# A mixer and mixture-of-experts kernel on one core: gate projection as one batch in other banks, output projection in two halves, the last units summed on VectorE, expert weights issued later, new due times

## The chip, the cores and the metric

The kernel runs on one core of a Trainium2 chip. The metric is the device time of one execution in microseconds (us). Five engines work side by side and each executes its own instructions in order: TensorE (PE in the profile; its weight loads are PEld), VectorE (DVE), ScalarE (ACT), GpSimd (POOL) and SyncE (SP), which here only issues transfers. Transfers (DMAs) run apart from the engines, once issued.

## The reference

The input is 16 sequences of 256 positions and 256 features, all float32. Cut to what matters:

```python
x = L0_attn_input_states                       # 16 x 256 x 256
xn = _layernorm(x, axis=-1)
x = x + _L0_attn_ref(xn, ...) + _L0_ffn_ref(xn, ...)

# _L0_attn_ref, a state-space mixer: E = 512 channels, N = 16 states, TR = 128
hidden, gate = jnp.split(jnp.einsum('blh,he->bel', input_states, W_in), 2, axis=1)
hidden = silu(depthwise_conv(hidden, conv_kernel) + conv_bias)       # 4 taps, causal
dt, Bm, Cm = jnp.split(hs_ble @ W_x, [TR, TR + N], axis=-1)
dts = softplus(dt @ W_dt + b_dt)
dA, dBu = exp(dts * A), dts * Bm * hs_ble
state = a * state + bu;  y = einsum('ben,bn->be', state, c)          # scan over positions
y = (scan_out + hidden * D) * silu(gate)
return jnp.einsum('bel,eh->blh', y, W_out)

# _L0_ffn_ref, 32 experts of width 96; the 8 largest router weights are kept
acc + ((silu(x @ wg) * (x @ wu)) @ wd) * w_e
```

## The kernel before

**Tiling.** A sequence (`b`, 0 to 15) is handled as a whole. Its normalized input is kept transposed (`xnT`: features on partitions, 256 positions along the free axis). Two branches read it.

The *mixer* branch: `project` makes the hidden half (4 blocks of 128 channels, in two calls), `conv_first` and `conv_rest` the convolution, `activate` its SiLU, `params` and `widen` and `steps` the step sizes. Its B and C rows go through DRAM (`keep_params`) and come back copied to all partitions (`fetch`, tile `rep`, three buffers). Then 16 units follow, 8 groups of two states (`g`) by 2 halves of the channels (`u`). A unit `k` is: `feed` on GpSimd (L622), for each of its two blocks `decay` on ScalarE (L636), `scan` on VectorE (L644) and `read` on VectorE (L654), and `collect` (L659), a GpSimd-issued transfer that adds the unit's product `pr` to the accumulator `y` as it lands. After the last group `fold` (GpSimd, L667) adds y's two states, `gate` (TensorE, L675) and `gate_silu` (ScalarE, L684) make the gate, `gated` (GpSimd, L689) multiplies, `project_out` (TensorE, L696) projects and `finish` (VectorE, L713) adds the result to the output tile.

The *expert* branch: all 32 experts are computed as 24 blocks of 128 rows, in 12 pairs `q`. `gates` makes two pairs at a time (L469, tile `pg`), `silu` (L482) empties both, `ups` makes one pair (L469, tile `pu`), `weigh` (GpSimd, L488) applies router weights that were spread over partitions (`spread`, L455), `combine` (VectorE, L492) multiplies with the ups, and `down` (L504) accumulates the pair into one PSUM bank `acc`. `settle` (L709) adds that to the output tile, `store` (L717) writes it.

**PSUM banks.** They are rings: two banks `g`, two banks `u`, one `acc`, three for the scan's `da`. A step that takes a bank waits for the bank's owner two turns earlier. In the kernel before the g banks serve `gates`, the first half of `project` and of `widen`, the router's products, `params` and a few small ones; the u banks serve `ups`, the second half of `project` and of `widen`, `turn`, `gate` and `project_out`.

**Order.** Nothing is scheduled by the chip. A planner written into the kernel (`Plan`, L20 to L117) plays the engines forward in time at build: each step has an engine, a length, steps that it needs, ring buffers that it takes and gives, and a due time; a free engine takes the ready step with the smallest due time. The order it arrives at is the program order of each engine. ScalarE needs another function table for exp, SiLU, softplus and square root; a step that needs no change of table counts as due `STAY` us earlier. `early` keeps a step from being planned sooner than so long before it is due. Due times are one base per sequence (`ORIGIN + PERIOD * b` for the mixer, `ORIGIN + LEAD + RATE * b` and a share of it for the experts) plus an offset per kind of step (`DUE`, and `FIRST` for sequence 0). Times in the plan only make the order: on the chip a step runs when its engine reaches it and what it waits for is done.

The weights are loaded once and stay. `load_experts` (L286, L282) loads the experts' weights in four parts of 8 experts, each part in three kinds, 20 transfers on SyncE's queue in all.

Of the kernel before, what the change touches and what calls it, by code (L numbers as in the profile page):

```python
# [19 lines left out]
class Plan:  # L20
# [10 lines left out]
    STAY = 3.0  # L31
# [89 lines left out]
def mamba_moe_kernel(  # L121
# [57 lines left out]
    ORIGIN = 6.0  # L179
    PERIOD = 81.5  # L180
    RATE = 82.5

    DUE = dict(
        load_x=-118.0, stats=-76.5, root=-82.5, invert=-118.5, norm=-68.5, turn=-129.0,
        keep_turned=-72.0, route=-80.5, largest=-63.5, expo=-63.5, choose=-77.0,
        turn_weights=-84.5, keep_weights=-110.5, project=-56.5, conv_first=-44.5, conv_rest=-58.5,
        activate=-57.5, params=-66.0, keep_params=-43.5, widen=-53.0, steps=-31.5, skip=-22.0,
        clear=-38.5, inputs=-11.5, fetch=17.0, feed=-4.5, decay=-6.5, scan=8.5, read=-14.6,
        collect=3.5, spread=2.0, gates=-16.5, ups=10.5, silu=2.5, weigh=-3.5, combine=-3.0,
        down=17.0, settle=76.0, gate=60.0, gate_silu=36.0, fold=84.0, gated=88.5, project_out=84.5,  # L190
        load_again=87.5, finish=40.5,
    )
    EARLY = dict(
        load_x=59.0, stats=5.0, turn=45.0, route=11.0, project=19.0,
# [3 lines left out]
        route=5.0, largest=-13.0, expo=-10.0, choose=-13.0, turn_weights=-18.0, keep_weights=-10.0,  # L198
        project=-4.0, conv_first=3.5, conv_rest=-16.0, activate=-20.0, params=-10.5,
        keep_params=-12.0, widen=-23.0, steps=-0.5, skip=17.5, clear=1.0, inputs=21.5, fetch=8.0,  # L200
        feed=-6.0, decay=-3.0, scan=3.0, read=-6.0, collect=2.5, spread=-10.5, gates=-2.5,
        ups=-5.5, silu=2.5, weigh=2.0, combine=10.0, down=-0.5,
    )
    LEAD = -8.0
# [459 lines left out]

    def fold(b, u):
        y = live["y", b, u]
        nc.gpsimd.tensor_add(y[:, :, 0, :], y[:, :, 0, :], y[:, :, 1, :])  # L667


    def gate(b, q):  # L670
        xs = live["xnT", b]
        pg = bank(f"pgate_{b}_{q}", "u").rearrange("p (j l) -> p j l", j=2)
        for j in range(2):
            for hc in range(HC):
                nc.tensor.matmul(  # L675
                    pg[:, j, :], win_sb[:, hc, E + (2 * q + j) * P : E + (2 * q + j + 1) * P],
                    xs[:, hc, :],
                    start=(hc == 0), stop=(hc == HC - 1),
                )
# [243 lines left out]
```

## Time and profile before

| | |
|---|---|
| time, median of 3 runs (lowest to highest) | 1373.9 us (1372.63 to 1378.73) |
| time of the profiled execution | 1376.13 us |
| span of the profile, first to last instruction | 1374.3 us |
| granted TensorE clock, mean over the span | 0.988 |
| TensorE matmuls busy | 1307.1 us, 6000 instructions |
| VectorE busy | 1161.8 us |
| ScalarE busy | 1125.8 us |
| GpSimd busy | 1191.5 us |

Each float32 matmul stands as two instructions in the profile, so one `ups` or one `down` (4 matmuls) is a row of x8, one `gates` (8 matmuls) a row of x16. In answers on groups and waits a line of the kernel and its tiles name the step (`pu<-xnT,wu_sb` at L469 is `ups`). A wait is written "who waits <- what it waited for: us in all, times, longest". In the timeline a row is its start, its duration, the engine and the step, with the idle time of the engine before it in brackets.

### The profile page before, as it was taken

What the parts mean: (1) busy time and instruction counts of PE and PEld (TensorE: products, weight loads), DVE (VectorE), ACT (ScalarE), POOL (GpSimd) and SP (SyncE); (2) the same over time, 40 slices, a digit from 0 to 9 for tenths busy, and PEclk for the clock granted to TensorE, in tenths of its full rate; (3) what the DMA queues carried; (4) which work ended last, traced back from release to release, by engine and by line L of the source; (5) the groups of instructions that cost most, each with busy time, mean ns of one, the idle gap of its engine ahead of it and who ended that gap; (6) DMA issues with size and microseconds to landing.
All of it is one profiled execution on the core that took longest, in us unless ns stands there. A gap on an engine that the chain in (4) does not pass through costs nothing.

```text
span 1374.3 us, 18848 instructions
## 1 busy us (share of the span) xinstructions
PE 1307.1 (95%) x6000; PEld 1111.7 (81%) x6000; DVE 1161.8 (85%) x1729; ACT 1125.8 (82%) x1905; POOL 1191.5 (87%) x839
## 2 busy tenths in 40 slices
PE   7898899999999999999999999999999999999997
PEld 5777777787788888878888888888888888888875
DVE  2598878988899798888989888898888989888984
ACT  4688798697988979888888988879798887988863
POOL 0688978888899899989898998989899898998985
PEclk8999999999999999999999999999999999999997
DMA  8998978889889989998899999899998999988895
GB/s 247 257 223 176 230 164 196 188 204 220 177 194 225 193 198 214 203 206 184 208 215 208 195 205 203 203 210 212 201 202 195 206 205 214 200 211 191 193 223 100
DMA packets 165875, 278.22 MB, mean 202 GB/s; under 512 B 33008, under 2 KB 99600, under 8 KB 165776
## 3 DMA queue, kind: packets, MB, share of 16 engines
q0 software_dynamic: 36864, 134.23, 51.3%
q1 hardware_dynamic: 126272, 142.74, 37.8%
q8 instruction: 47, 0.77, 0.2%
q10 hardware_dynamic: 2640, 0.05, 0.1%
q14 instruction: 52, 0.43, 0.1%
HBM read 137.51 MB, written 5.24 MB: 104 GB/s over the span
## 4 chain that ended last, share of the span: by engine, by line
POOL 29%; DVE 18%; DMA 15%; PE 12%; ACT 11%; issue 10%; SPq 4%; POOLq 0%; ACTq 0%; DVEq 0%
POOL bu L622 11%; POOL sg L488 8%; DVE da L644 7%; DMA rep<-bcd 7%; POOL y L659 5%; DVE hs L536 4%; DVE pr L654 4%; ACT da L636 4%; PE pu L469 3%; DMA y<-pr 3%; SPq L455 3%; PE acc L504 3%; DMA wr<-wd 3%; POOL y L667 2%; PE pg L469 2%
## 5 line engine op out<-in xcount | busy, mean ns | idle before, releaser
L622 POOL TENSOR_TENSOR bu<-rep,hs 128x1024 f32<-128x1024 f32 x256 | 717.2, 2990 | 113.2 <-DVE da L644 72.2
L644 DVE TENSOR_TENSOR_SCAN da<-da,bu 128x512 f32<-128x512 f32 x512 | 607.9, 1217 | 83.3 <-ACT da L636 56.1
L636 ACT ACTIVATE da<-dts,a_sb 128x256 f32<-128x256 f32 x1024 | 470.9, 473 | 145.6 <-DVE pr L654 124.6
L469 PE MATMUL pu<-xnT,wu_sb 128*128 128x256 f32 x1536 | 362.2, 383 | 24.0 <-ACT gs L684 15.3
L659 POOL DMA_DIRECT2D y<-pr x256 | 360.4, 1413 | 15.8 <-DVE pr L654 7.3
L504 PE MATMUL acc<-wd_sb,h 128*128 128x256 f32 x1536 | 361.6, 379 | 3.3 <-DVE h L492 3.0
L469 PE MATMUL pg<-xnT,wg_sb 128*128 128x256 f32 x1536 | 351.4, 382 | 13.2 <-DVE hs L536 4.8
L469 PEld LDWEIGHTS pu<-xnT,wu_sb 128*128 128x128 f32 x1536 | 291.0, 191 | 70.2 <-ACT gs L684 20.2
L469 PEld LDWEIGHTS pg<-xnT,wg_sb 128*128 128x128 f32 x1536 | 292.0, 191 | 59.8 <-ACT da L636 7.9
L654 DVE TENSOR_TENSOR pr<-da,rep 128x512 f32<-128x512 f32 x512 | 333.3, 676 | 7.3 <-DMA y<-pr 5.2
L488 POOL TENSOR_TENSOR sg<-sg,wr 128x512 f32<-128x512 f32 x192 | 309.2, 1949 | 34.6 <-DMA wr<-wd 33.7
L504 PEld LDWEIGHTS acc<-wd_sb,h 128*128 128x128 f32 x1536 | 290.1, 190 | 44.3 <-DVE h L492 4.7
L492 DVE TENSOR_TENSOR h<-pu,sg 128x512 f32<-128x512 f32 x192 | 130.9, 682 | 75.8 <-PE pu L469 37.9
L636 ACT ACT_TABLE_LOAD x140 | 179.6, 1283 | 2.5
L482 ACT ACTIVATE sg<-pg 128x512 f32<-128x512 f32 x192 | 104.3, 593 | 6.4 <-PE pg L469 3.9
L482 ACT ACT_TABLE_LOAD x82 | 105.2, 1283 | 1.5
L536 DVE SCALAR_TENSOR_TENSOR hs<-ph,small,hs 128x255 f32<-128x255 f32 (+2 forms) x192 | 88.7, 478 | 11.2 <-ACT hs L527 6.6
L696 PE MATMUL po<-wout_sb,y 128*128 128x256 f32 x256 | 63.9, 405 | 8.2 <-POOL y L689 8.2
L667 POOL TENSOR_TENSOR y<-y 128x512 f32<-128x512 f32 x32 | 65.2, 2038 | 1.2 <-DMA y<-pr 1.2
L689 POOL TENSOR_TENSOR y<-y,gs 128x512 f32<-128x512 f32 x32 | 65.8, 2075 | 0.2
L696 PEld LDWEIGHTS po<-wout_sb,y 128*128 128x128 f32 x256 | 51.4, 204 | 17.4 <-POOL y L689 10.0
L551 PE MATMUL px<-hs,wx_sb 128*32 128x256 f32 (+1 forms) x256 | 63.1, 395 | 2.3 <-ACT wT L439 2.3
(64 smaller groups left out, 809.2 us busy)
## 6 DMA issues: line engine op xcount, KB each, us to landing
y<-pr POOLq DMA_DIRECT2D x256, 512.0 KB, 7.4
rep<-bcd SPq DMA_DIRECT2D x128, 512.0 KB, 6.2
wr<-wd SPq DMA_DIRECT2D x128, 192.0 KB, 4.7
wr<-wd SPq DMA_DIRECT2D x128, 128.0 KB, 5.9
wr<-wd SPq DMA_DIRECT2D x128, 64.0 KB, 5.1
xt<-L_attn_input_states_dram SPq DMA_DIRECT2D x16, 256.0 KB, 8.0
o<-L_attn_input_states_dram SPq DMA_DIRECT2D x16, 256.0 KB, 7.5
out_dram<-o SPq DMA_DIRECT2D x16, 256.0 KB, 6.3
```

The lines of the kernel that those rows point to most:

```text
L469: nc.tensor.matmul(p[:, j, :], w[:, hc, ts(c, P)], xs[:, hc, :], start=(hc == 0), stop=(hc == HC - 1),)
L482: nc.scalar.activation(sg, live.pop(("g", b, q)), AF.Silu)
L488: nc.gpsimd.tensor_mul(sg, sg, wr[:, r : r + 2, :])
L492: nc.vector.tensor_mul(h, live.pop(("u", b, q)), live.pop(("sg", b, q)))
L504: nc.tensor.matmul(acc[:, s, :], h[:, j, ts(s, P)], wd_sb[:, c, :], start=(c == 0 and s == 0), stop=(c == FC - 1), skip_group_check=True,)
L536: nc.vector.scalar_tensor_tensor(cv[:, c, k:], ph[:, j, : L - k], cw[:, c, KC - 1 - k : KC - k], cv[:, c, k:], op0=ALU.mult, op1=ALU.add,)
L622: nc.gpsimd.tensor_mul(bu, live["rep", b, g][:, 0:1].to_broadcast([P, CPU, NG, L]), live["hs", b][:, ts(u, CPU), :].unsqueeze(2).to_broadc ...
L636: nc.scalar.activation(da[:, i, :], dts[:, c, :], AF.Exp, scale=a_sb[:, c, n : n + 1])
L644: nc.vector.tensor_tensor_scan(flat, flat, live["bu", k][:, j].rearrange("p n l -> p (n l)"), 0.0, op0=ALU.mult, op1=ALU.add,)
L654: nc.vector.tensor_mul(live["pr", k][:, j], live.pop(("da", m)), live["rep", b, g][:, 1])
L659: nc.gpsimd.dma_start(live["y", b, u].rearrange("p c n l -> p (c n l)"), live.pop(("pr", k)).rearrange("p c n l -> p (c n l)"), accum_op=A ...
L696: nc.tensor.matmul(po[:, s, :], y[:, c % CPU, 0, ts(s, P)], wout_sb[:, c, :], start=(c == 0), stop=(c == EC - 1),)
```

## The change

- `gate` is one step of both halves, 16 matmul instructions, and takes the two g banks in place of two u banks one after the other; `gate_silu` empties both banks in one step.
- `project_out` is two steps, one for each half of the channels, 8 matmul instructions each, in the same bank. Except for the last sequence, the first half still needs both `gated` steps. The order of accumulation inside is by channel block, then by position half.
- In the last sequence and the last group (two units), `collect` is no transfer: VectorE adds the two states of `pr` and adds the sum to `y`, and `gated` is on VectorE too. `fold` then comes ahead of that and needs only the group before.
- `load_experts` is due about 22 us later (the first at 0.6 where it was at -22.0), at the pace of the experts (RATE), and may not be planned more than 1 us before it is due.
- The second halves of `project` and `widen` are planned behind the first.
- `STAY` goes from 3.0 to 10.6; bases and all offsets of the due times are other numbers, and the last sequence has offsets of its own (`LAST`).

```diff
-    STAY = 3.0
+    STAY = 10.6
...
-    ORIGIN = 6.0
-    PERIOD = 81.5
-    RATE = 82.5
+    ORIGIN = 3.0
+    PERIOD = 81.9
+    RATE = 82.3
...
-        clear=-38.5, inputs=-11.5, fetch=17.0, feed=-4.5, decay=-6.5, scan=8.5, read=-14.6,
-        collect=3.5, spread=2.0, gates=-16.5, ups=10.5, silu=2.5, weigh=-3.5, combine=-3.0,
-        down=17.0, settle=76.0, gate=60.0, gate_silu=36.0, fold=84.0, gated=88.5, project_out=84.5,
-        load_again=87.5, finish=40.5,
...
+        clear=-29.0, inputs=-48.5, fetch=-80.5, feed=-8.5, decay=-1.5, scan=3.0, read=-126.1,
+        collect=-35.5, spread=-43.5, gates=-54.0, ups=64.5, silu=5.0, weigh=-76.0, combine=-3.0,
+        down=64.5, settle=-53.5, gate=39.5, gate_silu=95.5, fold=97.0, gated=11.0,
+        project_out=65.5, load_again=45.0, finish=4.0,
     )
     EARLY = dict(
-        load_x=59.0, stats=5.0, turn=45.0, route=11.0, project=19.0,
+        load_x=43.0, load_experts=1.0, stats=5.0, turn=43.0, route=125.0, project=149.0,
     )
...
+    LAST = dict(
+        fetch=64.5, feed=83.5, decay=37.0, scan=-2.5, read=-160.5, collect=-14.0, spread=53.0,
+        gates=7.5, ups=210.0, silu=46.5, weigh=277.0, combine=-108.5, down=-39.5, settle=62.0,
+        gate=-7.0, gate_silu=-383.5, fold=314.5, gated=6.0, project_out=-95.5, finish=14.0,
+    )
-    LEAD = -8.0
+    LEAD = -2.4
...
+    def collect_last(k):
+        b, g, u = unit(k)
+        pr, y = live.pop(("pr", k)), live["y", b, u]
+        nc.vector.tensor_add(pr[:, :, 0, :], pr[:, :, 0, :], pr[:, :, 1, :])
+        nc.vector.tensor_add(y[:, :, 0, :], y[:, :, 0, :], pr[:, :, 0, :])
+
+    def gated_last(b, q):
+        y = live["y", b, q][:, :, 0, :]
+        nc.vector.tensor_mul(y, y, live.pop(("gs", "gate", b, q)))
...
-    def gate(b, q):
+    def gate(b):
         xs = live["xnT", b]
-        pg = bank(f"pgate_{b}_{q}", "u").rearrange("p (j l) -> p j l", j=2)
...
+        for q in range(EC // 2):
+            pg = bank(f"pgate_{b}_{q}", "g").rearrange("p (j l) -> p j l", j=2)
...
-    def project_out(b):
-        po = bank(f"po_{b}", "u").rearrange("p (s h) -> p s h", s=SPS)
-        for s in range(SPS):
-            for c in range(EC):
-                y = live["y", b, c // CPU]
+    def project_out(b, u):
+        if u == 0:
+            live["po", b] = bank(f"po_{b}", "u").rearrange("p (s h) -> p s h", s=SPS)
+        po, y = live["po", b], live["y", b, u]
+        for j in range(CPU):
+            for s in range(SPS):
+                c = CPU * u + j
                 nc.tensor.matmul(
-                    po[:, s, :], y[:, c % CPU, 0, ts(s, P)], wout_sb[:, c, :],
-                    start=(c == 0), stop=(c == EC - 1),
+                    po[:, s, :], y[:, j, 0, ts(s, P)], wout_sb[:, c, :],
+                    start=(c == 0 and s == 0), stop=(c == EC - 1), skip_group_check=True,
                 )
...
+        due += LAST.get(kind, 0.0) if b == B - 1 else 0.0
...
-            due = ORIGIN + LEAD + PERIOD / PARTS * j + 4.0 * i - 20.0
+            due = ORIGIN + LEAD + RATE / PARTS * j + 4.0 * i
...
-            add("collect", (k,), "POOL", 0.61, at + PERIOD / SLOTS, k,
-                needs=[("read", CPU * k + j) for j in range(CPU)] + [("clear", b)]
-                + ([("collect", k - PAIRED)] if g else []), gives=[("pr", k)], lands=7.0)
+            reads = [("read", CPU * k + j) for j in range(CPU)]
+            if b == B - 1 and g == GROUPS - 1:
+                add("collect", (k,), "DVE", 1.25, at + PERIOD / SLOTS, k, fn=collect_last,
+                    needs=reads + [("fold", b, u)], gives=[("pr", k)])
+                continue
+            add("collect", (k,), "POOL", 0.61, at + PERIOD / SLOTS, k,
+                needs=reads + [("clear", b)] + ([("collect", k - PAIRED)] if g else []),
+                gives=[("pr", k)], lands=7.0)
...
+        add("gate", (b,), "PE", 8 * MM, t, b, gives=[xT],
+            takes=[(r, (r, "gate", b, q)) for q in range(2) for r in ("g", "gs")],
+            needs=[("keep_turned", b)] + ([] if b else [("load_in", 1)]), early=10.0)
+        add("gate_silu", (b,), "ACT", 1.09, t, b, needs=[("gate", b)],
+            gives=[("g", "gate", b, q) for q in range(2)], table="silu")
         for q in range(2):
...
+            k = UNITS * b + UNITS - PAIRED + q
+            end = b == B - 1
+            add("fold", (b, q), "POOL", 1.23, t + 2.0 * q - (12.0 if end else 0.0), b, q,
+                needs=[("collect", k - PAIRED if end else k)])
+            add("gated", (b, q), "DVE" if end else "POOL", 0.6 if end else 1.23, t + 2.0 * q, b, q,
+                needs=[("collect", k) if end else ("fold", b, q), ("gate_silu", b)],
+                gives=[("gs", "gate", b, q)], fn=gated_last if end else gated)
+        for q in range(PAIRED):
+            add("project_out", (b, q), "PE", 4 * MM, t + 2.0 * q, b, q,
+                needs=[("gated", b, q)] + ([("project_out", b, q - 1)] if q else [] if end else [("gated", b, q + 1)])
+                + ([] if b else [("load_out",)]),
+                takes=[] if q else [("u", ("po", b))], gives=[("y", b, q)])
```

## The prediction

> **What bounds the kernel now.** I read the page first, then busy time by stretches, the waits, and the timeline at two places. The page says that TensorE is the fullest engine by far, and where it isn't: the first slices and the last.
>
> ```profile
> span 1374.3 us, 18848 instructions
> PE 1307.1 (95%) x6000; PEld 1111.7 (81%) x6000; DVE 1161.8 (85%) x1729; ACT 1125.8 (82%) x1905; POOL 1191.5 (87%) x839
> ...
> PE   7898899999999999999999999999999999999997
> ...
> PEclk8999999999999999999999999999999999999997
> ```
>
> Busy time by stretches (length, then busy us and instructions of PE, PEld, DVE, ACT, POOL, then clock, DMA share, GB/s) gives the size of it. The row of 81.50 us is one full period in the middle: TensorE busy 80.08, so it lacks 1.42. From 60 to 400 us it lacks 4.7, 3.1, 5.7, 4.1, 6.8 and 4.5, in all 28.9 us, where the middle (1.4 in 100) would lack 4.8. That is 24 us more than the middle's rate.
>
> ```profile
> 60.00:80.00 20.00, 15.29 (x70) 11.76 (x69) 19.14 (x38) 13.39 (x26) 17.20 (x13) 1.00 1.08 271
> 80.00:100.00 20.00, 16.90 (x78) 14.21 (x76) 18.42 (x26) 18.48 (x33) 19.24 (x14) 1.00 0.94 207
> 100.00:150.00 50.00, 44.28 (x193) 37.36 (x193) 39.98 (x52) 39.76 (x65) 43.06 (x30) 0.97 0.86 188
> 150.00:200.00 50.00, 45.94 (x213) 37.81 (x214) 40.73 (x70) 42.57 (x71) 41.36 (x30) 1.00 0.92 209
> 200.00:300.00 100.00, 93.16 (x422) 78.23 (x421) 85.32 (x121) 82.55 (x141) 87.45 (x62) 0.98 0.83 187
> 300.00:400.00 100.00, 95.53 (x436) 81.28 (x435) 88.38 (x130) 83.70 (x143) 89.44 (x64) 0.98 0.89 199
> ...
> 780.40:861.90 81.50, 80.08 (x375) 68.84 (x375) 72.60 (x109) 70.30 (x120) 74.37 (x53) 1.00 0.91 205
> ```
>
> The waits name the 1.42: ups wait for a u bank that the gate's SiLU has to empty, 12 times, 3.0 us of it once near the end.
>
> ```profile
> PE pu L469 <- ACT gs L684: 15.3, 12, 3.0
> ```
>
> The timeline shows one such place: gate holds both u banks from 775.53, ScalarE comes to its SiLU at 779.77, TensorE stands 1.27 us. It also shows how long the g banks are held: gates from 772.08, emptied by the SiLU that ends at 787.36.
>
> ```profile
> 772.08 3.62 PE L469 MATMUL pg<-xnT,wg_sb 128*128 128x256 f32 x16
> 775.53 3.62 PE L675 MATMUL pgate<-xnT,win_sb 128*128 128x256 f32 x16
> 779.77 1.08 ACT L684 ACTIVATE gs<-pgate 128x512 f32<-128x512 f32 x2
> 780.42 3.72 PE L469 MATMUL pu<-xnT,wu_sb 128*128 128x256 f32 x16 [1.27 <-ACT gs L684]
> 786.28 1.08 ACT L482 ACTIVATE sg<-pg 128x512 f32<-128x512 f32 x2
> ```
>
> The tail: the last read ends at 1357.37, the store is issued at 1371.17, 13.8 us later, by way of a transfer, fold, gated and a projection at half speed (12 instructions in 5.49 us).
>
> ```profile
> 1356.68 0.69 DVE L654 TENSOR_TENSOR pr<-da,rep 128x512 f32<-128x512 f32 x1
> 1357.66 0.85 POOL L659 DMA_DIRECT2D y<-pr  x1 [2.19 <-DVE pr L654]
> 1362.27 1.26 POOL L667 TENSOR_TENSOR y<-y 128x512 f32<-128x512 f32 x1 [0.49 <-DMA y<-pr]
> 1363.61 1.26 POOL L689 TENSOR_TENSOR y<-y,gs 128x512 f32<-128x512 f32 x1
> 1364.92 5.49 PE L696 MATMUL po<-wout_sb,y 128*128 128x256 f32 x12 [1.02 <-POOL y L689]
> 1370.45 0.69 DVE L713 TENSOR_TENSOR o<-po,o 128x512 f32<-128x512 f32 x1 [12.13 <-PE po L696]
> 1371.17 0.38 SPq L717 DMA_DIRECT2D out_dram<-o  x1
> ```
>
> **The change part by part**, against the profiled execution's own 1376.1 us (span 1374.3), which is 2.2 above the median 1373.9.
>
> *Gate in the g banks.* The matmuls stay (16 in 3.6 us), the SiLU too (two in 1.08 us, already adjacent). What goes is the ups' wait: 15.3 less the 3.0 near the end, 12.3 us on TensorE, which sets the period. With both u banks free, two ups (3.7) and a down (1.9) can cover the 1.6 us from the gate's last matmul (779.15) to the SiLU's end. Late next: gates, which now wait for gate_silu, and gate, which waits for the silu before it. I take 12.3, bounds 0 and 12.3.
>
> *Last units on VectorE.* After the last read: two additions and a multiplication at 0.68 (the rate of 128x512 rows on VectorE), 2.0; 8 matmuls; finish 0.69. With 0.6 for handovers and the matmuls at half speed, 3.5 (8 took 3.53 after the 2.95 us wait at 1340.24; at full speed 1.9), that is 6.8 where 13.8 was. y isn't ready at once: the group before's transfer for this half was issued at 1350.02 to 1352.38, landing takes 7.4, fold 1.26, so about 1359; the addition waits some 0.9 us. Gain 6.1. VectorE's queue holds the second unit's scan and read, combine and settle behind the first unit's collect, and that one waits for its fold: if its transfer lands 2 to 3 us late, all of these slip. At best the matmuls run at full speed and fold is early, 8.7; at worst 3. The 3.0 wait and the slow matmuls at 1340.24 (1.6 more) are worth nothing alone, since the experts (1357.6) and the reads (1357.4) end together: 0, at most 4.6.
>
> *A rule against this part.* Alone, fold takes 1.26 us; its mean over the run is 2.04 where VectorE is busy. The Trainium skill, "SBUF — State Buffer", section "Who interferes with whom", says that a VectorE instruction with two inputs in SBUF contends with GpSimd's reads, and the new additions have both there, where read has one in PSUM. By this rule two folds might collide, and the part would be worth 2 x 1.26 less, 3.6; by the rows it is 6.1. Which of them holds the chain stays open.
>
> *Weights held back.* 20 issues on SyncE move behind the bcd and wr issues, the first rep fetch, load_x of sequence 1. In the first 50 us, GpSimd's first feed waits 3.3 us for rep, and SyncE issued expert loads for 1.1 and 2.2 us between bcd and that fetch: a gain up to 3.3. Against it, a part that lands after TensorE wants it costs up to one landing, 7.1 us by the wg row, for three parts 21. TensorE reaches the second `gates` at 33 us, so a part due near 21 is in time: I take 0, bounds -21 and +3.3.
>
> *Due times, STAY, the ordering of project and widen, project_out in halves.* They alter only the order. project_out's 16 instructions stay and, before the last sequence, both halves still need both gated: 0. Table loads (302 of 1.283 us, 387 of ScalarE's 1126) may fall, but ScalarE has 11 us free in a period: 0; that cover goes if SiLU is put off, which is the second rival. The 24 us excess of 60 to 400 us is what an order could win. No row shows which of these waits goes. An order as good as the middle's gains 24, one that adds two thirds of it again loses 15; I take +8, a third of the excess.
>
> Sum: 12.3 + 6.1 + 0 + 8 = 26.4, so 1349.7 against the profiled execution, 1347.5 against the median. **Forecast 1348.**
>
> **The rivals.** *Another engine keeps the period.* GpSimd is busy 74.4 of 81.5 and waits some 7 (for VectorE 6.3 in that period); VectorE 72.6. If feed, scan, read and the bu buffers close a ring of 81.5, TensorE only waits elsewhere and the tail alone is won: 1373.9 - 6.1 = 1368; with a little of the start, 1366. For it: the period is constant and GpSimd near 91%. Against it: TensorE's only long wait in the period is the gate's.
>
> *The g banks become the bound; the other side.* In the period of the timeline the six gates batches hold them 15.3, 4.7, 10.1, 6.5, 4.7 and 5.4 us, 46.7 in all; route, weights, params, one project, one widen and root hold one bank each for 30 bank-us, 15 of both. The gate adds 5.3 (775.53 to 780.85): 67 of 80. Room for seven batches is 13, 1.9 us each. From there on it decides, and each tenth more costs 0.7 us a period. STAY can do it: a SiLU may be passed over 7.6 us of due time longer. At 2.2 us longer, the period is 1 us above the old one: 16 lost, tail won: 1373.9 + 16 - 6.1 = 1384. Against it: ScalarE idles about 11 us a period, mostly waiting for VectorE, and would take a SiLU then.
>
> *The weights come late.* 1373.9 + 21 - 6.1 - 12.3 = 1376: a change that shows no gain.
>
> The clock is told by rows: after 2.95 and 4.2 us of waiting the matmuls ran at 0.43 us, after 1.27 us at 0.22. The Trainium skill, "TensorE: Matmul & The Clock Gate", section "What's actually happening", gives an idle window of about 3.4 us for the slow state; by it, the last half of project_out would run at full speed wherever its wait stays under that, and the tail gain would be 7.7.
>
> **How the numbers follow.** Forecast 0.55, its own range 1326 (gate 12.3, tail 8.7, start 24 and weights 3.3 off 1373.9) to 1365 (gate 5, tail 3, start 1 off). Another engine 0.17, g banks 0.20, late weights 0.08. A measurement of this kernel tells about 0.5%, 7 us: below 1367 is faster, above 1381 slower. Faster: 0.55 + 0.12 of the 0.17 = 0.67; same: the rest of that and late weights, 0.13; slower: 0.20, the g banks. The range 1327 to 1385 leaves out the ends of the first case and the upper half of the g banks' case.
>
> **What would show it.** Gate: no wait of ups for gs, matmul periods near 80.1 us. Tail: from the last read to the store 6 to 8 us. Start: TensorE lacks less than 24 us between 60 and 400. Table loads fewer than 302. Wrong if TensorE's waits move to gates (for the SiLU or gs) with a period over 81.5, if GpSimd's busy share nears all of the period, if TensorE waits on wg, wu or wd in the first 80 us, or if VectorE stands before the last additions for fold.

## The result, and the profile after

The changed kernel takes 1392.8 us (median; 1385.4 to 1395.5), the kernel before 1374.8 us beside it: ratio 1.0119, 95% interval 1.0074 to 1.0165. The change made the kernel 1.2% slower, and the time lies above the upper end of the predicted range, 1385. The profiled execution takes 1395.5 us (before 1376.1), with a mean granted clock of 0.978 of full speed (before 0.988).

The page of the changed kernel: span and instructions, busy time of each engine, then TensorE's busy share and its granted clock in 40 slices.

```profile
span 1393.8 us, 18885 instructions
PE 1310.6 (94%) x6000; PEld 1119.4 (80%) x6000; DVE 1163.9 (84%) x1735; ACT 1125.3 (81%) x1902; POOL 1187.4 (85%) x835
...
PE   8768999999999999999999898998989989999988
...
PEclk9889999999999999999999999999999999999999
```

Three things are to be seen. TensorE's slices 5 to 22 all stand at 9; from slice 23 on, 8 alternates with 9, so something recurs there that the kernel before did not have. The clock of the last slice is 9 where it was 7. And the busy sums hardly move (TensorE 1307.1 to 1310.6 us), so most of the 19.5 us of span are waiting, not work.

The waits of the changed kernel (engine, line, what it waited for: us in all, times, longest):

```profile
POOL bu L628 <- DVE da L650: 102.5, 23, 10.6
DVE h L498 <- POOL sg L494: 71.4, 28, 4.8
DVE st L346 <- DMA xt<-L_attn_input_states_dram: 64.9, 10, 11.9
...
PE acc L510 <- DVE h L498: 41.6, 11, 10.7
...
PE pg L475 <- DVE hs L542: 9.2, 7, 1.5
```

Three of these waits in the kernel before:

```profile
DVE st L340 <- DMA xt<-L_attn_input_states_dram: 3.8, 1, 3.8
PE acc L504 <- DVE h L492: 3.0, 3, 2.1
PE pg L469 <- DVE hs L536: 4.8, 7, 1.9
```

The ups' wait for the gate's SiLU, 15.3 us before, is gone, as forecast. Three others have grown. VectorE waits 64.9 us for the input of the next sequence (`xt`), where it waited 3.8 us, once, before. TensorE's `down` waits 41.6 us for `combine` (`h`), 3.0 before. The gates wait 9.2 us for `hs`, 4.8 before: for the g bank that `project`'s first half holds until `conv_rest` has read it.

The view of tile `xt` gives how long the load itself takes, from issue to landing, in the kernel before and, below it, in the changed kernel:

```profile
DMA to landing us min/median/max: 3.1/8.0/10.6
DMA to landing us min/median/max: 3.0/8.6/11.7
```

The load is little slower: for sequences 10 to 15 it takes 9.8 to 11.7 us, where it took 7.1 to 10.6. What changed is when it is issued. Before, from sequence 2 on, load_x went out 26 to 56 us ahead of its `stats`, and nothing waited but sequence 0. Now, for sequences 10 to 15, it goes out only 1 to 7 us ahead of the moment at which VectorE comes to `stats`, and for sequence 2 behind it. One such place in the timeline of the changed kernel (start, us, engine, line, what; in brackets the idle time before it and its releaser):

```profile
767.96 0.40 SPq L616 DMA_DIRECT2D rep<-bcd  x1
768.40 0.47 SPq L240 DMA_DIRECT2D xt<-L_attn_input_states_dram  x1
...
770.37 0.69 DVE L660 TENSOR_TENSOR pr<-da,rep 128x512 f32<-128x512 f32 x1
...
780.14 0.75 DVE L346 BATCH_NORM_STATS2 st<-xt 128x6 f32<-128x256 f32 x2 [9.08 <-DMA xt<-L_attn_input_states_dram]
...
782.14 0.67 DVE L498 TENSOR_TENSOR h<-pu,sg 128x512 f32<-128x512 f32 x1
...
782.32 2.34 POOL L628 TENSOR_TENSOR bu<-rep,hs 128x1024 f32<-128x1024 f32 x1 [3.64 <-DVE da L650]
...
782.87 3.78 PE L510 MATMUL acc<-wd_sb,h 128*128 128x256 f32 x8 [5.83 <-DVE h L498]
```

The load is issued at 768.40 and VectorE is free at 771.06. It stands 9.08 us in front of `stats`, and behind `stats` in its queue are a scan, `combine` and a read. `combine` runs at 782.14; TensorE stands 5.83 us until it has, and its next eight matmuls take 3.78 us where eight take 1.89 elsewhere. `feed` on GpSimd waits for the scan 3.64 us. One late load of 256 KB stops three engines.

Busy time by stretches (length, then busy us and instructions of PE, PEld, DVE, ACT, POOL, then clock, DMA share, GB/s):

```profile
60.00:80.00 20.00, 17.30 (x72) 13.57 (x71) 19.13 (x38) 13.50 (x26) 11.90 (x9) 0.91 0.96 231
80.00:100.00 20.00, 9.34 (x36) 7.64 (x36) 8.06 (x14) 8.02 (x14) 8.63 (x7) 0.76 0.81 204
100.00:150.00 50.00, 46.31 (x212) 40.05 (x211) 44.42 (x57) 43.42 (x71) 47.16 (x34) 0.99 0.98 212
150.00:200.00 50.00, 48.10 (x228) 40.61 (x227) 44.91 (x73) 41.05 (x75) 43.26 (x30) 1.00 0.86 199
200.00:300.00 100.00, 97.56 (x449) 83.98 (x448) 89.46 (x129) 86.95 (x146) 94.25 (x68) 0.98 0.92 206
300.00:400.00 100.00, 98.03 (x459) 84.31 (x459) 85.09 (x128) 87.19 (x147) 91.29 (x66) 1.00 0.88 200
578.00:659.00 81.00, 79.78 (x374) 68.85 (x374) 72.03 (x109) 70.51 (x119) 73.39 (x51) 1.00 0.91 205
782.90:871.20 88.30, 81.98 (x374) 70.18 (x374) 72.55 (x109) 70.81 (x119) 74.26 (x53) 0.96 0.82 188
```

From 100 to 400 us TensorE lacks 10.0 us where it lacked 21.1: the start did get better. From 60 to 400 us it lacks 23.4 where it lacked 28.9, just under the 24 that the prediction named as its sign. The row of 80 to 100 us shows a first wait for `xt` (11.9 us, sequence 2). The two last rows are full periods: 81.0 us without a wait for `xt` and 88.3 with one, at the same number of instructions.

The tail in the timeline of the changed kernel, cut to what ends it:

```profile
1380.32 1.27 POOL L684 TENSOR_TENSOR y<-y 128x512 f32<-128x512 f32 x1 [1.19 <-DMA y<-pr]
1380.39 1.75 DVE L676 TENSOR_TENSOR y<-y,pr 128x512 f32<-128x512 f32 x1
...
1382.06 0.68 DVE L660 TENSOR_TENSOR pr<-da,rep 128x512 f32<-128x512 f32 x1
...
1388.00 1.89 PE L719 MATMUL po<-wout_sb,y 128*128 128x256 f32 x8
...
1389.92 0.69 DVE L735 TENSOR_TENSOR o<-po,o 128x512 f32<-128x512 f32 x1 [1.03 <-PE po L719]
1390.64 0.39 SPq L739 DMA_DIRECT2D out_dram<-o  x1
```

From the end of the last read (1382.74) to the store are 7.9 us, where there were 13.8, and the projection runs at full speed.

Where the time went is seen from the start of the last matmul instruction of each sequence's `down`, read off the trace (sequences counted from 0; the last column is the end of the span). `e1` is the first experiment below.

| | seq 3 | seq 7 | seq 12 | seq 15 | end |
|---|---|---|---|---|---|
| before | 391.0 | 719.5 | 1127.0 | 1357.2 | 1374.3 |
| after | 382.4 | 709.3 | 1149.1 | 1387.8 | 1393.8 |
| after less before | -8.6 | -10.2 | +22.1 | +30.6 | +19.5 |
| e1 | 377.8 | 702.7 | 1112.7 | 1350.4 | 1356.4 |

The changed kernel is 10 us ahead by sequence 7, loses 32 from there to sequence 12, where the loads of sequences 10 to 14 are waited for (9.1, 9.5, 8.6, 8.2 and 8.6 us; sequence 10's is the one in the timeline, at 768 us, while an earlier sequence's experts run), loses 8.5 more, with sequence 15's wait of 4.0 us among it, and wins 11.1 behind the last `down`.

`down` is the experts' step, and the new order shifts the experts against the mixer: the last `down` ended 0.2 us behind the last read before, and now ends 5.4 us behind it. So the mixer's own measure belongs beside it. By the end of the last read of sequences 3, 7, 12 and 15 the changed kernel is 6.6 and 6.9 us ahead, then 22.7 and 25.4 behind, and wins 5.9 us from the last read to the end; `e1` is 11.2, 13.3, 10.4 and 11.5 us ahead, and 17.9 at the end.

### The profile page after: what moved, and what is told of

The parts are those of the page before. It is cut to its first block, busy times and chain, and to the rows that moved or that the text cites. A ratio compares the mean times of both kernels' runs of the same rounds, so it can differ in the third digit from the quotient of the medians.

```text
span 1393.8 us, 18885 instructions
## 1 busy us (share of the span) xinstructions
PE 1310.6 (94%) x6000; PEld 1119.4 (80%) x6000; DVE 1163.9 (84%) x1735; ACT 1125.3 (81%) x1902; POOL 1187.4 (85%) x835
## 4 chain that ended last, share of the span: by engine, by line
DMA 28%; POOL 20%; DVE 18%; PE 16%; issue 10%; ACT 4%; SPq 3%; ACTq 0%; POOLq 0%; DVEq 0%
DMA y<-pr 12%; POOL sg L494 8%; DVE da L650 7%; DMA rep<-bcd 7%; POOL bu L628 6%; PE acc L510 5%; DMA xt<-L_attn_input_states_dram 5%; PE pu L475 4%; PE pg L475 4%; POOL y L665 4%; DVE pr L660 4%; DVE hs L542 3%; SPq L461 2%; DVE h L498 2%; PE pgate L693 1%
## 5 line engine op out<-in xcount | busy, mean ns | idle before, releaser
L628 POOL TENSOR_TENSOR bu<-rep,hs 128x1024 f32<-128x1024 f32 x256 | 774.0, 3113 | 117.5 <-DVE da L650 102.5
L510 PE MATMUL acc<-wd_sb,h 128*128 128x256 f32 x1536 | 378.2, 391 | 41.8 <-DVE h L498 41.6
L510 PEld LDWEIGHTS acc<-wd_sb,h 128*128 128x128 f32 x1536 | 298.4, 196 | 89.5 <-DVE h L498 47.2
L475 PE MATMUL pg<-xnT,wg_sb 128*128 128x256 f32 x1536 | 352.7, 383 | 13.5 <-DVE hs L542 9.2
L475 PEld LDWEIGHTS pu<-xnT,wu_sb 128*128 128x128 f32 x1536 | 291.8, 191 | 55.4 <-DVE h L498 11.1
L494 POOL TENSOR_TENSOR sg<-sg,wr 128x512 f32<-128x512 f32 x192 | 310.6, 1951 | 23.8 <-DMA wr<-wd 23.4
L684 POOL TENSOR_TENSOR y<-y 128x512 f32<-128x512 f32 x32 | 81.6, 2550 | 1.2 <-DMA y<-pr 1.2
L709 POOL TENSOR_TENSOR y<-y,gs 128x512 f32<-128x512 f32 x30 | 72.4, 2414 | 0.0
L346 DVE BATCH_NORM_STATS2 st<-xt 128x6 f32<-128x256 f32 x32 | 12.0, 417 | 64.9 <-DMA xt<-L_attn_input_states_dram 64.9
L521 PE MATMUL ph<-xnT,win_sb 128*128 128x256 f32 x256 | 62.7, 390 | 1.2 <-DVE h L498 1.2
```

The lines of the kernel that those rows point to most:

```text
L475: nc.tensor.matmul(p[:, j, :], w[:, hc, ts(c, P)], xs[:, hc, :], start=(hc == 0), stop=(hc == HC - 1),)
L494: nc.gpsimd.tensor_mul(sg, sg, wr[:, r : r + 2, :])
L510: nc.tensor.matmul(acc[:, s, :], h[:, j, ts(s, P)], wd_sb[:, c, :], start=(c == 0 and s == 0), stop=(c == FC - 1), skip_group_check=True,)
L628: nc.gpsimd.tensor_mul(bu, live["rep", b, g][:, 0:1].to_broadcast([P, CPU, NG, L]), live["hs", b][:, ts(u, CPU), :].unsqueeze(2).to_broadc ...
```

## The experiments

Theory A: the loss is load_x's place on SyncE's queue. These are its due times in the change (lines cut at the dots):

```diff
-        load_x=-118.0, stats=-76.5, ...
+        load_x=-47.0, stats=-98.5, ...
...
-        load_x=59.0, stats=5.0, ...
+        load_x=43.0, load_experts=1.0, stats=5.0, ...
```

The second pair says by how much a step may be planned ahead of its due time. So the earliest time of load_x in the plan went from t-177 to t-90 (t is its sequence's base time), while that of `stats` went from t-81.5 to t-103.5. The planner counts 2.9 us from issue to landing (256 KB at 280 KB in a us, and 2.0); the median in the changed kernel is 8.6. Theory B: the new order of the middle (gates waiting for `conv_rest`) sets the time. Theory C: the weights held back cost the start.

Edits to an order need care here, since the planner moves everything when one step changes. Most kernels below therefore take the order that the planner gave and move single steps within it; `move(name, at)` takes a step out of the list and puts it in front of the first that starts later than `at`, in planned us.

**load_x alone, 20 us earlier** (`e1_x_earlier`, from the changed kernel):

```diff
+        for b in range(2, 16):
+            move(("load_x", b), where["load_x", b]["start"] - 20.0)
```

> The changed kernel; only the load of the next sequence's input (load_x, sequences 2 to 15) stands about 20 us of planned time earlier in SyncE's queue. Every other queue is unchanged. Theory A (VectorE stands in stats for a load that was issued too late, and everything behind it in its queue is late): the wait of stats for xt falls from 64.9 us to under 5, the periods of 87 to 88 us after 780 us go back to about 81, the 10.8 us stall of TensorE near 97 us goes; time 1340 to 1350. Rival (the new order is bad in itself, VectorE only waits somewhere else): time stays above 1380.

Measured: 1359.0 us, ratio to the kernel before 0.9895 (0.9878 to 0.9911), 33.9 us less than the changed kernel, and faster than both. In its waits view, these lines tell what is left:

```profile
DVE h L510 <- POOL sg L506: 109.6, 38, 8.0
...
PE pg L487 <- DVE hs L554: 17.0, 13, 1.5
PE pu L487 <- DVE h L510: 16.0, 3, 7.7
...
DVE st L358 <- DMA xt<-L_attn_input_states_dram: 3.9, 1, 3.9
```

The one wait for `xt` is sequence 0's, as before. Nothing but SyncE's order was edited, so some 34 us of the changed kernel's time was load_x's place (33.0 if each of the two is taken against the runs of the kernel before that stand beside it). A stands, but the time is some 10 us above what it expected. In the middle, the gates wait for `hs` once a period, and combine for the weighted `sg` that GpSimd makes (109.6 us in all, where it was 35.4 in the kernel before).

From sequence 7 to 12 its periods are still 81.4 to 82.6 us, where 80.1 was forecast.

**The reverse, in the kernel before** (`e3_before_x_late`, then `e5_before_x_short`): the kernel's old order, load_x put 3.1 us of planned time ahead of `stats`; the second also puts `stats` directly behind it in VectorE's order.

```diff
+        for b in range(2, 16):
+            move(("load_x", b), where["stats", b]["start"] - 3.1)
+            st = where["stats", b]                                  # e5 only
+            seq.remove(st)                                          # e5 only
+            seq.insert(seq.index(where["load_x", b]) + 1, st)       # e5 only
```

> The kernel before; only load_x of sequences 2 to 15 stands later in SyncE's queue, 3.1 us of planned time ahead of stats where it was 26 to 48. Theory A: stats waits for xt 5 to 9 us in most of the 14 sequences, 50 to 110 us in all, and the time rises by 30 to 80 us. Rival (such a wait is covered by VectorE's slack of 9 us a period): the time stays within 7 us of 1374.

> The kernel before; load_x of sequences 2 to 15 stands 3.1 us of planned time ahead of the old place of stats, and stats stands directly behind it in VectorE's queue, some 3 us earlier than it was. Theory A: stats waits for xt 30 to 70 us in all, and the time rises by half of that, 15 to 35 us. Rival (such waits are covered by VectorE's slack): within 6 us of 1374.

Measured: e3 1377.2 us, 1.0025 (1.0013 to 1.0037); e5 1398.3, 1.0175 (1.0153 to 1.0198). In e3, VectorE waited for `xt` only 12.7 us in 6 places, 3.8 of it for sequence 0: on the chip it comes to `stats` later than planned, so the real lead was about 8.5 us in most sequences, a little over the landing of 7.4 (median). The edit was too weak. In e5 the lead is gone, and the waits view shows

```profile
DVE st L355 <- DMA xt<-L_attn_input_states_dram: 37.0, 14, 6.3
```

37.0 us of waits, 33 of them new, and 23.6 us of time, with no other part of the change in the kernel. This agrees with A from the other side. It is the weaker test of the two: e5 also moves `stats` up in VectorE's order, and what that alone costs was not tried, while e1 edits SyncE's order and nothing else.

**The planner told the landing** (`r1_lands8`): in the changed kernel, `lands=2.0` of load_x becomes 8.0, and the planner orders everything anew.

> The changed kernel, ordered anew by its planner with one number mended: the load of the next input is planned to land 8 us after its transfer (measured median 8.6 from issue) where it was 2.0. Theory A: stats waits for xt under 15 us in all, time 1345 to 1365. Rival (the other due times no longer fit, since a new plan moves every queue): the xt waits go but other waits replace them, time 1370 or more.

Measured: 1364.7 us, 0.9934 (0.9914 to 0.9954); the waits for `xt` fall from 64.9 to 11.0. So one constant, mended by 6 us, gives 28 of the 34 us, though in a new plan, in which other steps have moved too.

**The gates' wait for `conv_rest`** (theory B): `e2_x_conv_earlier` puts conv_rest directly behind conv_first on top of e1, `f1_x_finish_conv` puts the finish of the sequence before ahead of both.

```diff
+        for b in range(2, 16):
+            at = seq.index(where["conv_first", b, 0]) + 1
+            row = [where["conv_rest", b, 0, 0], where["conv_rest", b, 0, 1]]
+            fin = [st for st in seq[at:] if st["name"][0] == "finish"][:1]     # f1 only
+            if fin and seq.index(fin[0]) < seq.index(row[1]):                  # f1 only
+                row = fin + row                                                # f1 only
+            for st in row:
+                seq.remove(st)
+            seq[at:at] = row
```

The lines are f1's; e2's own lines do the same without the two that are marked.

> As the kernel with the earlier load, and besides the convolution's additions on the first half of the channels (conv_rest of the half that holds a g bank, sequences 2 to 15) stand directly behind the ScalarE step that feeds them, ahead of two reads and a finish in VectorE's queue. Theory B (the gate's wait was replaced by one of gates for that g bank, 1.3 to 1.5 us a period): these waits go, a period is near 80.0 us, time 12 to 20 us under the kernel with the earlier load alone. Rival (GpSimd or VectorE keeps the period at 81.5): the waits move on, time within 5 us of that kernel.

> As the kernel with the earlier load; in VectorE's queue finish and then conv_rest of the half that holds a g bank stand directly behind the ScalarE step that feeds conv_rest, so that neither holds a bank longer than now (in the kernel with conv_rest alone moved, ups waited 31.8 us for finish). Theory B (the gate's wait was replaced by one of gates for the g bank that project holds): the waits of gates for hs fall from 17 us to under 5, no other TensorE wait takes their place, a period is 80 to 80.5 us, time 12 to 20 us under the kernel with the earlier load, so 1340 to 1347. Rival (a third wait takes their place): time within 5 us of it, 1354 to 1364.

Measured: e2 1377.7 us, 18.7 more than e1; f1 1367.9, 9.0 more. The waits view of e2:

```profile
PEld pu L492 <- DVE o L752: 37.4, 14, 3.8
PE pu L492 <- DVE o L752: 31.8, 14, 3.4
```

and of f1:

```profile
PE pu L496 <- ACT dts L610: 6.6, 12, 0.6
PE acc L531 <- DVE h L519: 6.3, 10, 2.9
```

In both, the gates' wait for `conv_rest` went (17.0 us in e1). In e2 the ups then wait for the u bank that finish, pushed behind conv_rest, has to empty. In f1 that went too, and smaller waits for other things took its place, with periods of 81.5 to 83.5 from sequence 7 to 12. Taking a wait away from TensorE gained nothing twice, but both edits also push other steps of VectorE back. So what sets the period is asked directly.

**Work taken out, TensorE and GpSimd** (`h2_x_less_down` and `h1_x_no_fold` from e1, `k2_before_less_down` and `k1_before_no_fold` from the kernel before). h2 and k2 leave out 256 matmul instructions of `down`, h1 and k1 the fold of 15 sequences; their results lack what these make.

```diff
-        for j in range(2):                                  # down: h2, k2
+        for j in range(1 if q in (1, 4, 7, 10) else 2):
```

```diff
-        nc.gpsimd.tensor_add(y[:, :, 0, :], y[:, :, 0, :], y[:, :, 1, :])       # fold: h1, k1
+        if b == B - 1:
+            nc.gpsimd.tensor_add(y[:, :, 0, :], y[:, :, 0, :], y[:, :, 1, :])
```

> The kernel with the earlier load; four of the twelve pairs of a sequence leave out the second block in down, so the experts' sum lacks four of 24 blocks: 16 matmul instructions, 3.45 us less on TensorE in a period. If TensorE sets the period: it falls by 3 us or more and the time by 40 to 55 us. If GpSimd or the ring of feed, scan and read sets it: the period stays within 0.7 us and the time within 12 us of 1359.

> The kernel with the earlier load; fold is left out in sequences 0 to 14, so the second state's half of each unit is missing from their results: 2.5 us less on GpSimd in a period. If GpSimd sets the period of 81.5: it falls to 79 to 80.5 and the time by 15 to 35 us, to 1325 to 1345. If TensorE with its order sets it: the period stays within 0.4 us and the time within 6 us of 1359.

> The kernel before, in its own order; four of the twelve pairs of a sequence leave out the second block in down: 3.45 us less on TensorE in a period, 55 in all. If TensorE sets the period, as the prediction took it: time 40 to 55 us under 1374. If GpSimd sets it: within 8 us of 1374.

> The kernel before, in its own order; fold is left out in sequences 0 to 14, so the second state's half of each unit is missing from their results: 2.5 us less on GpSimd in a period. If GpSimd sets the period in the kernel before too: time 10 to 25 us under 1374. If TensorE sets it, as the prediction took it: within 5 us of 1374.

Measured: TensorE's busy time fell from 1300.1 to 1263.4 us in h2 and from 1307.1 to this in k2:

```profile
PE 1263.5 (92%) x5744; PEld 1060.6 (77%) x5744; DVE 1160.0 (84%) x1729; ACT 1125.3 (82%) x1905; POOL 1191.3 (87%) x839
```

It gave nothing, in h2 (1359.8 against 1359.0) and in k2 (1376.2, 1.0013 of the kernel before, 0.9998 to 1.0028). Leaving out the fold of 15 sequences gave 16.5 us in h1 (1342.4) and 17.9 in k1 (1356.5, 0.9875, 0.9848 to 0.9902); k1's middle period is 80.6 instead of 81.5, and h1's periods from sequence 4 to 14 are 80.9 in the mean instead of 81.9. The same 500 us of the kernel before, of k2 and of k1, in that order:

```profile
700.00:1200.00 500.00, 491.51 (x2297) 422.68 (x2296) 444.86 (x661) 432.46 (x732) 455.90 (x320) 1.00 0.91 204
```

```profile
700.00:1200.00 500.00, 474.83 (x2197) 401.77 (x2196) 443.13 (x660) 431.56 (x730) 455.19 (x319) 1.00 0.90 203
```

```profile
700.00:1200.00 500.00, 495.18 (x2320) 427.71 (x2319) 450.62 (x666) 436.46 (x735) 448.00 (x312) 1.00 0.92 207
```

With a hundred matmuls fewer in the stretch (x2197), the other engines do what they did: TensorE, busy 98% of the time, did not hold the period. With the fold gone TensorE, VectorE and ScalarE do more in the same time. So what sets the period goes through the fold on GpSimd, at least in part, and not through TensorE's work. It is not simply GpSimd's time: thirty folds at their mean of 2.04 us are 61 us, and 18 came back.

**Is it GpSimd's total work, or where the fold stands?** `i2_x_clear_vector` moves another operation of GpSimd, the memset of `clear`, to VectorE; `i1_x_fold_vector` moves the fold itself, both in e1, for sequences 1 to 15 and 0 to 14.

```diff
-            nc.gpsimd.memset(live["y", b, u][:, :, 1, :], 0.0)                      # i2
+            (nc.vector if b else nc.gpsimd).memset(live["y", b, u][:, :, 1, :], 0.0)
```

```diff
-        nc.gpsimd.tensor_add(y[:, :, 0, :], y[:, :, 0, :], y[:, :, 1, :])           # i1
+        eng = nc.gpsimd if b == B - 1 else nc.vector
+        eng.tensor_add(y[:, :, 0, :], y[:, :, 0, :], y[:, :, 1, :])
```

> The kernel with the earlier load; clear (two memsets of 1.0 us as recorded) is on VectorE in sequences 1 to 15, at the place in the order that it had; nothing is left out. If GpSimd's time sets the pace: 4 to 12 us under 1359. If not, or if VectorE then stands for skip: 1357 to 1365.

> The kernel with the earlier load; fold is on VectorE in sequences 0 to 14, at the place in the order that it had: 2.5 us less on GpSimd, 1.4 more on VectorE in a period; nothing is left out. If GpSimd's time sets the period and VectorE has room for it (72 of 81.5 busy): 1340 to 1352. If VectorE then stands for the transfers that fold waits for, or its own load binds: 1355 to 1370.

Measured: i2 1361.3 us, 0.9897 (0.9883 to 0.9912), the same as e1, so moving GpSimd's thirty memsets of 1 us, which take 0.49 us each on VectorE, won nothing. i1 1384.7, 1.0083 (1.0055 to 1.0111), 25.8 more than e1. The view of the fold's line in i1 (ns min/median/max, first and last start):

```profile
L697 DVE TENSOR_TENSOR y<-y x30: 672/1338/6129, 144.6 to 1310.2; 128x512 f32<-128x512 f32 x30
```

An addition of 0.67 us took 1.34 at the median and 6.13 at worst, and VectorE's busy time rose by 69 us for 30 operations, of which 20 would be their own. Each of the thirty ran after its unit's transfer had landed and beside GpSimd's work, so it is not a wait for the transfer. The fold cannot be handed to VectorE, and i1 tells nothing of GpSimd's sum of work, since VectorE lost more than GpSimd won. i2 speaks against that sum, but doesn't settle it: GpSimd's busy time fell by 14 us, and VectorE's rose by as much. That the fold matters and the memset doesn't fits the fold's place in GpSimd's queue, between the transfer that it waits for and the feeds behind it; this was not tested, and which steps close the ring of 81.5 us is not settled by these runs.

**The weights** (theory C): `e4_x_weights_earlier` moves parts 1 to 3 of the expert weights 18 us of planned time earlier on top of e1, `f2_x_weights23_earlier` parts 2 and 3 only. `i3_x_last_weights_late` moves the last `down` part behind a fetch.

```diff
+        for j in range(1, 4):           # e4; range(2, 4) in f2
+            for kind in "gud":
+                move(("load_experts", j, kind), where["load_experts", j, kind]["start"] - 18.0)
```

> As the kernel with the earlier load, and besides parts 1 to 3 of the experts' weights stand 18 us of planned time earlier in SyncE's queue, about where they were before the change. If holding the weights back costs (parts land late, TensorE starves in the first 80 us), this is 5 to 20 us faster than the kernel with the earlier load alone; if holding them back helps the first fetch, it is 3 to 10 us slower; if neither, within 3 us.

> As the kernel with the earlier load; only parts 2 and 3 of the experts' weights stand 18 us of planned time earlier in SyncE's queue, part 1 stays. In the kernel that moved part 1 too, TensorE waited 19.7 us for part 0's ups weights that part 1 had overtaken. If holding parts 2 and 3 back costs (their transfers stand ahead of the rep fetch for which GpSimd's feed waits 10.4 us near 97 us), this is 4 to 10 us faster than 1359; if it helps, 3 to 10 slower; if neither, within 3.

> The kernel with the earlier load; only the last part of the down weights (768 KB) stands behind the sixth and seventh rep fetch in SyncE's queue. In the kernel with the earlier load this transfer was issued for 5.8 us right ahead of them, GpSimd's feed waited 10.4 us for rep near 97 us and TensorE 7.7. If that wait is worth its price: 4 to 10 us under 1359. If the start is made up for later: within 3 us.

Measured: e4 1367.6, 0.9953 (0.9938 to 0.9968), 8.6 more than e1; f2 1363.3, 0.9921 (0.9906 to 0.9936), 4.4 more; i3 1360.1, 0.9902 (0.9879 to 0.9925), no difference from e1. In e4, part 1 overtook the ups' part 0, and TensorE waited 19.7 us for it once, so its 8.6 is not the price of holding back; f2 is nearer to that, some 4 us, though its interval and e1's just touch. In i3 a wait of TensorE near 97 us fell from 7.75 to 3.94, and the time did not follow: C is out; holding back seems to help a little.

**The tail alone** (`g1_before_tail_fixed`): the kernel before in its own order, with the last two units collected and gated on VectorE, the fold put ahead of each and the halves of project_out behind each `gated`.

```diff
+        for q in range(2):
+            k = 254 + q
+            where["collect", k]["fn"], where["gated", 15, q]["fn"] = self.last
+            seq.remove(where["fold", 15, q])
+            seq.insert(seq.index(where["collect", k]), where["fold", 15, q])
```

> The kernel before, in its own order; only in the last sequence the last two collects and gated are done on VectorE at the places they had, fold stands ahead of each, and the two halves of project_out stand behind each gated. Prediction on record for this part: 6.1 us (3 to 8.7), so 1365 to 1371; from the last read to the store 6 to 8 us where it was 13.8. Rival (VectorE's additions contend with GpSimd or delay the last scans): 1372 to 1376.

Measured: 1370.4 us, 0.9976 (0.9960 to 0.9992), 3.1 us won at the median. The profiled execution is the slowest of ten (1376.2; they go from 1366.5) and wins nothing. Its timeline shows what eats the gain:

```profile
1355.75 1.27 POOL L705 TENSOR_TENSOR y<-y 128x512 f32<-128x512 f32 x1 [2.08 <-DMA y<-pr]
1355.86 1.70 DVE L683 TENSOR_TENSOR pr<-pr 128x512 f32<-128x512 f32 x1
1357.65 0.69 DVE L684 TENSOR_TENSOR y<-y,pr 128x512 f32<-128x512 f32 x1
1358.27 0.68 DVE L507 TENSOR_TENSOR h<-pu,sg 128x512 f32<-128x512 f32 x1
1358.87 1.22 DVE L659 TENSOR_TENSOR_SCAN da<-da,bu 128x512 f32<-128x512 f32 x1
...
1365.08 5.38 PE L698 MATMUL po<-wout_sb,y 128*128 128x256 f32 x16 [2.81 <-issue]
```

The first addition takes 1.70 us beside the fold (0.68 alone), and `combine` and the second unit's scan and read stand behind it. The last read ends at 1360.81, 3.4 us later than before (1357.37). From there to the store (1371.21) it is 10.4 us where it was 13.8, so just that much is won and lost. The projection's sixteen matmuls run together behind a wait of 2.81 us, and eight of them start 0.43 us apart where the others start 0.22: 5.38 us, where sixteen take 3.62 elsewhere.

**Parts alone, planned anew** (`f3_before_gate_only`, `f4_before_tail_only`): the gate's part and the tail's part put into the kernel before with its old due times, and the planner run again.

```diff
-        pg = bank(f"pgate_{b}_{q}", "u").rearrange("p (j l) -> p j l", j=2)
+            pg = bank(f"pgate_{b}_{q}", "g").rearrange("p (j l) -> p j l", j=2)
...
```

> The kernel before with one part of the change: gate as one batch in the g banks. Due times, STAY and all else as before, ordered anew by the planner. Prediction on record for this part: the wait of ups for gs (15.3 us) goes and nothing takes its place, 12 us faster, 1362. Theory B: the wait goes, but gates wait for a g bank instead, 10 to 20 us in all; time 1368 to 1380.

> The kernel before with one part of the change: last units summed and gated on VectorE and project_out in halves. Due times and all else as before, ordered anew by the planner. From the last read to the store 7 to 9 us where it was 13.8; time 4 to 8 us under 1374. Rival (VectorE's additions delay combine and the last scans by as much): time within 2 us of 1374.

Measured: 1477.8 (1.0752, 1.0735 to 1.0770) and 1438.8 (1.0469, 1.0438 to 1.0500). These isolate nothing. One changed step shifts the planner's choices on every queue; in f3 periods lay between 73 and 132 us. They show only that the old due times fit the old steps alone. What the gate's part is worth by itself, in a fixed order, was not tried.

## Why the prediction was wrong

**"They alter only the order" is the step that failed first.** The prediction costed the due times as a share of the excess of 60 to 400 us (+8, bounds +24 and -15) and looked at none of the due times singly. One of them added a wait: load_x may now leave no earlier than 13.5 us behind the earliest time of `stats` (t-90 and t-103.5), where it might leave 95.5 us ahead (t-177 and t-81.5), on a transfer that the trace of before shows taking 8.0. The due times stood in the change, the 8.0 in the page of the kernel before. By the planner's constant `stats` follows 2.9 us after the issue; 14 sequences at 8.0 less 2.9, 5.1 us each, would have been, as an estimate, 71 us on VectorE at worst, with `combine`, scan and read queued behind `stats`. e1 prices it at 34 us on the path, e5 at 24 in the old order. None of the rivals was this one; the slower end that the prediction did name, 1384 by the g banks, had another cause.

**The gate's 12.3 us: the wait went, the time did not.** "TensorE, which sets the period" is the failed step. No wait of ups for `gs` is left, and the period without `xt` waits is 81.0 to 82.5 in the changed kernel, not 80.1; in e1 the gates wait 1.3 to 1.5 us for `hs` once a period. k2 and h2 show the reason: take 44 and 37 us of busy time from TensorE and nothing comes back. The first rival, another engine keeps the period, was right for this part, and its sign, GpSimd at 74.4 of 81.5, stood in the row that the prediction quoted; k1 and h1 show that the fold on GpSimd has a part in it. The prediction gave that rival 0.17, because TensorE's only long wait in the period was the gate's. A wait says what an engine lacks, not that it would go faster without it. The Trainium skill, "Perfetto Trace Analysis", section "Identifying the Most-Contended Engine", warns that the matmul busy share is no good measure of how close TensorE is to its peak, since matmuls are pipelined, and names the weight-load busy share as one to use instead; here the weight loads were busy 68.84 of 81.50, 84%, under GpSimd's 91%, and k2 agrees with that reading, not with the 98%. These runs show that TensorE's work does not set the period; the gate's part alone, in a fixed order, they do not price.

**The tail: right, though alone it is smaller.** In the changed kernel 13.8 became 7.9 and in e1 7.4, within the 6 to 8 forecast: 5.9 and 6.4 us won, where 6.1 was taken. Alone, g1 gives 3.1, at the lower bound of 3. The term that was mis-sized there is the addition: 1.70 and 1.75 us beside the fold, where 0.68 was taken. The prediction had weighed that collision and named 3.6 for it, and in its list of what would make it wrong it named scan, read and combine behind the first unit's collect; that is what g1 shows. In the changed kernel the experts' last `down` and the last project_out end together, and the projection's matmuls ran at full speed, the prediction's best case; in g1 half of them ran at half speed. The 7.7 that the prediction worked out, with full speed behind any wait under 3.4 us, is not borne out: behind g1's wait of 2.81 us half of the matmuls ran slow.

**The start: somewhat more than taken.** +8 was taken; by the last read of sequence 7, 6.9 us were won in the changed kernel and 13.3 in e1, and what TensorE lacks from 60 to 400 us fell from 28.9 to 23.4 and 19.6. How much of it is due times, gate or weights was not separated. **The weights: 0 was taken;** f2 suggests some 4 won, i3 that putting the last `down` part behind the fetches changes nothing. **Table loads** are 299 where they were 302, and 0 was taken for them.

**The g banks as a bound** did not come in that size. Gates do wait for a g bank, but behind `conv_rest`, and removing that wait (f1) won no time.

Put together from the runs: without load_x's short lead the change stands at 1359.0, 15 us better than before. The profiled executions are 17.9 us apart. By the last reads, e1 is 13.3 ahead by sequence 7, gives back 5.0 by sequence 14, wins 3.2 in the last sequence and 6.4 behind its last read. The forecast of 1348 without the gate's 12.3 is 1360: near, but partly by luck, since the start gave 13.3 where 8 was taken and the middle cost 5.0 where nothing was taken; only the tail's 6.4 is the term as taken. What takes these 5 us, in periods of 82.2 in the mean from sequence 7 to 14 instead of 81.5, was not traced to one step.

## What to carry to other kernels

Read every due time that a change moves against the transfer that it releases: where the lead that is left is shorter than the landing that the trace shows (not the planner's constant), the first waiter stands, and all that is queued behind it. Here 61 us of such waits cost 34. Before a removed wait is counted as time won, find out whether its engine sets the period: leaving out some of its work is one run, and a busy share of 98% told nothing here. To try a part alone where a planner makes the order, keep the order and move single steps; a new plan is another kernel.

## What the runs showed of the hardware

- A load of 256 KB lands in 3.0 us at the start of the kernel, with little else in flight, and in 8.6 us at the median (up to 11.7) over the changed kernel, at a DMA busy share of 0.8 to 0.9; in e1, where it is issued earlier, in 6.8 (up to 9.2).
- A VectorE addition of 128x512 f32 with both inputs in SBUF takes 0.67 us alone, 1.70 and 1.75 beside one GpSimd addition of 1.27 us, and 1.34 at the median, 6.13 at most, spread over a run in which GpSimd is 83% busy (i1). Thirty of them added 69 us to VectorE's busy time.
- Eight matmuls behind a 5.83 us wait took 3.78 us, elsewhere 1.89; so this wait of TensorE cost 1.9 us more than its length. Shorter waits do so only sometimes. In the kernel before, sixteen matmuls of `gates` took 5.38 us behind a wait of 1.93 us, and 3.69, nearly their 3.62 at full speed, behind one of 3.00 us (start, us, step):

```profile
68.45 3.69 PE pg L469 x16
...
335.39 5.38 PE pg L469 x16
```
